# Four-layer graph network on one core: the third LSTM by seven products, an eigenvalue search from both ends, and a smaller arena placed by lifetimes

## The chip, the cores and the metric

The kernel runs on one core of a Trainium2 chip. The metric is device time in microseconds (us) of one execution; three executions of the kernel before took 2150.63, 2154.74 and 2155.52 us, so the median is 2154.74 us. The profile comes from one profiled execution. Engines are named as the profile names them: PE is the matmul engine (PEld its weight loads), DVE the vector engine, ACT the scalar engine, POOL GpSimd, SP the engine that issues most DMAs.

## What is computed

The input x is 128 graphs of 64 nodes with 256 features, and adj is one 64x64 matrix for all of them; everything is fp32. Four layers follow each other, each of the form x = x + layer(relu(layernorm(x))).

- **Layer 0** multiplies twice by adj and a 256x256 weight with a relu behind each, and then runs LSTMs with p = 0, 1, 2, 3 over windows of p + 1 nodes. The last hidden state of a window replaces the window's last node. Each step computes four gates:

```python
g = x_t @ Wih.T + h @ Whh.T + bias
i, f, gg, o = jnp.split(g, 4, axis=-1)
c = sigmoid(f) * c + sigmoid(i) * tanh(gg)
h = sigmoid(o) * tanh(c)
```

- **Layer 1** is graph attention with four heads and an MLP. Its first mix uses `2 * L / lam_max - I`, where lam_max is the largest eigenvalue of adj.
- **Layer 2** is one attention over the graph.
- **Layer 3** multiplies by the eigenvectors U of a 64x64 normalized Laplacian that is made from adj: U^T x, two small dense layers, U times the result.

The eigenvectors depend on adj alone. The kernel computes them itself, once, beside layer 0.

## The kernel before

**Tiling.** The 8192 rows (128 graphs of 64 nodes) are 64 tiles of 128 rows. Layer 0 takes them in NG = 8 groups of 8 tiles (`layer0`, line 1309), layers 1 to 3 in 16 groups of 4 tiles (`layer1` to `layer3`, lines 1523 to 1660). The result of layer 0 goes to DRAM (`put`) and is fetched back by the later groups.

**A planner sets the order.** No operation is issued as the Python text reaches it. `Plan.record` (line 114) notes each with its engine, its group and what it depends on; `Plan.schedule` (line 227) then goes through a simulated time with costs written out in `Plan.cost` (line 176) and, for each engine, picks an operation that can start earliest, with `Plan.rank` (line 328) to break ties; `Plan.issue` (line 338) emits all of them, in that fixed order. That one line, 344, is therefore the line of nearly all rows of the profile. Each engine works through its own list in order on the chip. `window` (line 968) lets at most two groups of layer 0 be in flight, then one group of the later layers beside the last group of layer 0, then eight. The groups have numbers: 0 to 7 are layer 0, then WEIGHTS, ATTN and REST to REST + 15 (layers 1 to 3).

**The eigenvalue work is a group apart.** It has the group number EIG and is named the plan's `aside` group. Its PE operations have rank -2, ahead of all others; its operations on DVE, ACT and POOL have rank 1000, so they fill what the groups leave. `eig_decomp` (line 347) brings the Laplacian to tridiagonal form in 62 steps, finds the eigenvalues by a search that counts sign changes of a Sturm sequence (line 634: NSWEEP = 9 sweeps, each with KS = 7 points for 3 levels, 21 numbers wide, over 64 partitions), and then makes the eigenvectors. In a sweep a loop over the 64 rows runs three DVE operations on 21 numbers each:

```python
for k in range(N):
    V.tensor_mul(PL[:, k + 1, :], DXf[:, k, :], PL[:, k, :])
    if k:
        b = W([N, 3, KS], 'b', 2)
        V.tensor_mul(b, PL[:, k - 1, :].rearrange('p (l s) -> p l s', l=3), E2[:, :, k - 1:k].to_broadcast([N, 3, KS]))
        V.tensor_sub(PL[:, k + 1, :], PL[:, k + 1, :], b.rearrange('p l s -> p (l s)'))
```

**LSTM steps.** `lstm_step` (line 1213) is the plain form: for each of 2 halves of the hidden features and 4 gates, two products with Wih and two with Whh into one PSUM bank (only Wih in a window's first step), then one ACT activation per gate and half. `lstm_fast` (line 1261) is Strassen's scheme in Winograd's form: each gate needs seven products with Wih and seven with Whh instead of eight and eight, each on half of the columns. `pieces` (line 1245) makes four extra right-hand sides, on POOL from the inputs and on DVE from the hidden state; four extra weight sums per matrix are made once by POOL at the start (line 1078) and stand in the tile `sums`. Between the products ACT copies banks out and DVE adds them. Before, p = 1 and p = 2 use `lstm_fast` in all steps but their first (line 1367). For p = 3 a group has 256 columns (2 halves of 8 tiles with 16 windows), and all four steps use `lstm_step`.

**Buffers.** There are 12 "big" buffers of 128x1024 fp32. Further ones come free later: 10 in `arena` when all EIG work is done (line 963), and 2, 7 and 5 in `Whh3`, `sums` and `mids` when layer 0 is done (lines 964 to 966), 36 in all. Before, `eig_decomp` lays its tiles side by side in the arena (10240 numbers per partition), with rings for some (`W`, line 372) and one region of 4080 that the stages share (`scope`, line 365).

**End of a group of layer 0.** Input x is fetched again for the residual sum (line 1374). `plan.behind` (line 1373) holds this fetch until the operation `last` has been issued; before, that is the last one ahead of p = 3. Sixteen PE transposes and four DVE adds of 128x512 end the group.

Of the kernel before, what the change touches and what calls it, by code (L numbers as in the profile page):

```python
# [8 lines left out]
ALU = mybir.AluOpType  # L9
AF = mybir.ActivationFunctionType  # L10
AX = mybir.AxisListType
# [4 lines left out]
KROW = 6  # L16
NEIG = 4080
EPS = 2.0 ** -24
# [50 lines left out]
class Plan:  # L69
# [258 lines left out]
    def rank(self, op):  # L328
        if op.group == self.aside:
            return (-2 if op.eng == "PE" else 1000, op.index)  # L330
        if op.eng == "SP":
            return (op.group, 0, op.index)
        g = min(max(op.group - op.lead, 0), self.ends)
        if op.group < REST:
            return (g, -op.lead, op.index)
        return (g, 6 * max(op.group - g, 0) - op.path, op.index)
# [10 lines left out]
def eig_decomp(plan, room, adj, adjT, ident, idf, ones):  # L347
# [14 lines left out]
    kept = {}  # L362
    inner = Carver(room.cut(NEIG))

    def scope():
        inner.reset([0])
        return inner

# [3 lines left out]
    def W(shape, name, bufs=None):  # L372

        if bufs is None:
            bufs = 2 if shape[-1] < N or name == "lab" else 1
        ring = kept.setdefault((name, tuple(shape)), [])
        if len(ring) < bufs:
            ring.append(room.tile(shape))
        else:
            ring.append(ring.pop(0))  # L380
        return ring[-1]

# [54 lines left out]
    V.memset(E[:, N - 1:N], 0.0)  # L437
    ph = scope()
    vb = [ph.tile([N, 2 * N]) for i in range(2)]
# [188 lines left out]
    C = 3 * KS  # L628
    ph = scope()
    PL = ph.tile([N, N + 1, C])  # L630
    V.memset(PL[:, 0, :], 1.0)
    DX = ph.tile([N, N, 3, KS])
    SG = ph.tile([N, N + 1, C])
    for s_ in range(NSWEEP):
        V.tensor_scalar(w, w, 1.0 / (KS + 1), None, op0=ALU.mult)
        x = W([N, 3, KS], 'x')
        V.tensor_scalar(x, c['ramp'], w, None, op0=ALU.mult)
        V.tensor_add(x, x, lo.unsqueeze(2).to_broadcast([N, 3, KS]))
        for l in range(3):
            V.tensor_mul(DX[:, :, l, :], BM[:, l, :].unsqueeze(2).to_broadcast([N, N, KS]), x[:, l, :].unsqueeze(1).to_broadcast([N, N, KS]))  # L640
            V.tensor_sub(DX[:, :, l, :], DM[:, l, :].unsqueeze(2).to_broadcast([N, N, KS]), DX[:, :, l, :])
        DXf = DX.rearrange('p k l s -> p k (l s)')
        for k in range(N):
            V.tensor_mul(PL[:, k + 1, :], DXf[:, k, :], PL[:, k, :])
            if k:
                b = W([N, 3, KS], 'b', 2)
                V.tensor_mul(b, PL[:, k - 1, :].rearrange('p (l s) -> p l s', l=3), E2[:, :, k - 1:k].to_broadcast([N, 3, KS]))
                V.tensor_sub(PL[:, k + 1, :], PL[:, k + 1, :], b.rearrange('p l s -> p (l s)'))
            if k % 8 == 7 and k < N - 1:
                mm = W([N, C], 'mm')  # L650
                V.tensor_reduce(mm, PL[:, k:k + 2, :].rearrange('p k c -> p c k'), op=ALU.max, axis=AX.X, apply_absolute_value=True)
                V.tensor_scalar(mm, mm, 1e-30, None, op0=ALU.max)
                V.reciprocal(mm, mm)
                V.tensor_mul(PL[:, k:k + 2, :], PL[:, k:k + 2, :], mm.unsqueeze(1).to_broadcast([N, 2, C]))
        V.tensor_scalar(SG, PL, 0.0, None, op0=ALU.is_lt)
        NE = DXf
        V.tensor_tensor(NE, SG[:, 1:, :], SG[:, :N, :], op=ALU.not_equal)
        ct = W([N, 3, KS], 'ct')
        V.tensor_reduce(ct.rearrange('p l s -> p (l s)'), NE.rearrange('p k c -> p c k'), op=ALU.add, axis=AX.X)
        V.tensor_tensor(ct, ct, li.unsqueeze(2).to_broadcast([N, 3, KS]), op=ALU.is_le)  # L660
        sm = W([N, 3], 'sm')
        V.reduce_sum(sm, ct, axis=AX.X)
        V.scalar_tensor_tensor(lo, sm, w, lo, op0=ALU.mult, op1=ALU.add)
# [6 lines left out]
    V.tensor_sub(dx, DM, dx)  # L670
    ph = scope()
    DQ = ph.tile([N, N, 2, 3])
# [202 lines left out]
    for _ in range(2):  # L875
# [8 lines left out]
        V.tensor_copy(Vc, pn[:N, N:2 * N])  # L884
    return AQf[:, N:], Vcf[:, :N], scope()

# [8 lines left out]
SETUP, WEIGHTS, ATTN, REST, EIG = -1, NG, NG + 1, NG + 2, 1000  # L895
NBIG, NMID, NSTAT, NATTN = 12, 10, 14, 4

# [32 lines left out]


@with_exitstack
def gnn_kernel(ctx: ExitStack, tc: tile.TileContext, a, out):
# [7 lines left out]

    arena = C([P, 10240], "arena")
    wih = [C([P, 2 * (3 if p == 0 else 4) * D], f"Wih{p}") for p in range(4)]
    whh = [None] + [C([P, 8 * D], f"Whh{p}") for p in range(1, 4)]
    sums = C([P, 2 * 7 * 4 * P], "sums")
    mids = C([P, NMID * 512], "mids")
# [130 lines left out]
    fastw = {}  # L1077
    for p in (1, 2):
        fastw[p] = []
# [24 lines left out]
    Ublk, UTblk = blockdiag(Ub), blockdiag(UTb)  # L1104
    room = Carver(arena)

    def colsum(col):

        pt = bank("colsum")
        PE.matmul(pt[:, :1], ones, col, start=True, stop=True)  # L1110
        r = room.tile([P, 1])
        V.tensor_copy(r, pt[:, :1])
        return r

    lam_j, lam_s = room.tile([N, N]), room.tile([P, 1])
    V.memset(lam_s, 0.0)

    def frob(m):
        V.scalar_tensor_tensor(lam_j, m, 1.0, m, op0=ALU.mult, op1=ALU.mult, accum_out=lam_s[:N])
        r = colsum(lam_s)  # L1120
        V.tensor_scalar(r, r, 1e-30, None, op0=ALU.max)
        G.tensor_tensor(r, r, mhalf[:, :1], op=ALU.pow)
        return r[:N]

    sym = room.tile([N, N])
    V.tensor_add(sym, adj2[:N], adjT2[:N])
    V.tensor_scalar(sym, sym, 0.5, None, op0=ALU.mult)
    Sf = room.tile([P, P])
    V.memset(Sf, 0.0)
    S = Sf[:N, :N]  # L1130
    V.scalar_tensor_tensor(S, sym, frob(sym), ident[:N, :N], op0=ALU.mult, op1=ALU.add)
    for i in range(21):
        pt = bank("lam_sq")
        PE.matmul(pt[:, :N], Sf, Sf[:, :N], start=True, stop=True)
        V.tensor_copy(S, pt[:N, :N])
        if i % 3 == 2:
            V.tensor_scalar(S, S, frob(S), None, op0=ALU.mult)
    V.scalar_tensor_tensor(lam_j, sym, 1.0, S, op0=ALU.mult, op1=ALU.mult, accum_out=lam_s[:N])
    lmax = colsum(lam_s)
    V.scalar_tensor_tensor(lam_j, S, 1.0, ident[:N, :N], op0=ALU.mult, op1=ALU.mult, accum_out=lam_s[:N])  # L1140
    den = colsum(lam_s)
    V.reciprocal(den, den)
    V.tensor_scalar(lmax, lmax, den, 1e-8, op0=ALU.mult, op1=ALU.add)
    V.reciprocal(lmax, lmax)
    V.tensor_scalar(lmax, lmax, 2.0, None, op0=ALU.mult)
    V.scalar_tensor_tensor(lapb, adjTb, lmax, ident, op0=ALU.mult, op1=ALU.subtract)


    QT, Vc, inner = eig_decomp(plan, room, adj2[:N], adjT2[:N], ident[:N, :N], ident, ones)
    for dst, lhs, rhs in ((Ublk, QT, Vc), (UTblk, Vc, QT)):  # L1150
        l2 = inner.tile([P, 2, N])
        V.tensor_copy(l2, lhs.unsqueeze(1).to_broadcast([P, 2, N]))
        pp = bank("U")
        PE.matmul(pp[:, :N], l2.rearrange("p r n -> p (r n)"), rhs, start=True, stop=True)
        V.tensor_copy(dst[0], pp[:N, :N])
        V.tensor_copy(dst[1], pp[N:, :N])

# [86 lines left out]

    def pieces(B, eng):

        n = B(0, 0).shape
        w = 1
        for k in n[1:]:
            w *= k  # L1250
        t = plan.value("big")[:, :4 * w].rearrange("p (i n) -> p i n", i=4)
        t = [t[:, i] for i in range(4)]
# [8 lines left out]
    def lstm_fast(p, xs, hs, cs, w, dsts):  # L1261


        R = [pieces(xs, G), pieces(hs, V)]
        sg = {}
# [43 lines left out]
    def layer0(fetched):  # L1309
# [47 lines left out]
        for p in range(1, 4):  # L1357
            k = p + 1
            nw = N // k
            if p == 3:  # L1360
                last = plan.ops[-1]
            for s in range(k):
                def win(c):
                    return hT[c].rearrange("p (b n t) -> p b n t", b=2, t=GT)[:, :, s:s + (nw - 1) * k + 1:k, :]
                ncol = 2 * GT * nw
                dst = win if s == p else lambda c: hs[:, c, :ncol]
                if s and p in (1, 2):
                    w = ncol // 2
                    lstm_fast(p, lambda c, n: win(c)[:, n], lambda c, n: hs[:, c, n * w:(n + 1) * w], cs, w, dst)
                else:  # L1370
                    lstm_step(p, s, win, hs, cs, ncol, dst)
# [55 lines left out]
    V.tensor_scalar(nb3a, nb3a, -1.0, None, op0=ALU.mult)  # L1427
    ursum = room.tile([P, 1])
    V.reduce_sum(ursum, Ub, axis=AX.X)
    V.tensor_scalar(b3b, b3b, ursum, None, op0=ALU.mult)  # L1430
    C3 = room.tile([P, P])
    pt = bank("ur")
# [279 lines left out]
```

## Time and profile before

| | us |
|---|---|
| median of three executions | 2154.74 |
| lowest, highest | 2150.63, 2155.52 |
| profiled execution: span from first to last instruction | 2149.3 |
| PE busy | 2102.0 (98%) |
| PE weight loads busy | 1665.0 (77%) |
| DVE busy | 1796.7 (84%) |
| ACT busy | 1124.1 (52%) |
| POOL busy | 708.4 (33%) |

For the profiled execution nothing but its span is given; the three timed executions lie 1.3 to 6.2 us above that span.

How to read it. The trace has two MATMUL records for one fp32 product and one for a transpose. [...] "Busy" is the time in which at least one record ran. A row of the table by form reads: line, engine, operation, output<-inputs, tile size, shapes, count, then busy us and mean ns of one, then the idle time of the engine ahead of these instructions and what ended it. A row of the table by stretches reads: from:to, its length, then PE, PEld, DVE, ACT and POOL with their busy us and counts, then the granted PE clock, the DMA share and GB/s. "big", "sums", "Wih" and other names are tiles; a later stage reuses such tiles under their old names, so `bank<-Whh,mids 128x128` is a product of layer 3.

### The profile page before, as it was taken

The numbers are of one execution on the slowest core, as the hardware profiler recorded it, in microseconds if no ns is written. First come the engines' busy times: TensorE is split into PE (matmuls) and PEld (weight loads), VectorE is DVE, ScalarE is ACT, GpSimd is POOL, SyncE is SP. The second block draws the span as 40 slices with busy tenths as digits, with TensorE's granted clock in tenths as the row PEclk, the third lists the DMA queues.
The fourth block names the chain that finished last, engine by engine and source line by source line (L and its number), as shares of the span: only waits on it lengthen the run. The fifth ranks groups of instructions, "written<-read, shape, count | busy, mean of one in ns | idle before, by whom it ended". The sixth has DMA issues, their size and how long they took to land.

```text
span 2149.3 us, 46200 instructions
## 1 busy us (share of the span) xinstructions
PE 2102.0 (98%) x16772; PEld 1665.0 (77%) x16772; DVE 1796.7 (84%) x7434; ACT 1124.1 (52%) x2465; POOL 708.4 (33%) x1040
## 2 busy tenths in 40 slices
PE   9999999999999999999999999999999999999998
PEld 6688688688778778778778788877777877887776
DVE  5788888888999999989989898767787789876787
ACT  3354354355345345345345444566667666665783
POOL 7211211310110110110110002696556657864353
PEclk9999999999999999999999999999999999999999
DMA  5000100100100100100000111200000100000001
GB/s 206 1 3 22 42 2 22 41 1 21 40 1 21 40 1 21 40 1 21 26 1 21 50 40 51 90 1 2 21 22 21 41 22 21 11 12 11 2 2 60
DMA packets 44868, 57.70 MB, mean 27 GB/s; under 512 B 8928, under 2 KB 38496, under 8 KB 44640
## 3 DMA queue, kind: packets, MB, share of 16 engines
q1 hardware_dynamic: 43536, 53.71, 7.6%
q8 instruction: 131, 2.15, 0.4%
q10 hardware_dynamic: 1104, 1.05, 0.2%
q14 instruction: 97, 0.79, 0.1%
HBM read 37.53 MB, written 16.78 MB: 25 GB/s over the span
## 4 chain that ended last, share of the span: by engine, by line
PE 79%; DVE 11%; POOL 3%; issue 3%; ACT 2%; DMA 2%; SPq 0%; DVEq 0%; ACTq 0%; POOLq 0%
PE bank L344 79%; DVE stat L344 3%; DVE arena L344 3%; DVE big L344 3%; POOL stat L344 2%; DVE mids L344 1%; DVE sums L344 1%; DMA big<-in_x_dram 1%; ACT big L344 1%; ACT mids L344 1%; POOL arena L344 0%; ACT arena L344 0%; POOL big L344 0%; DVE Whh L344 0%; SPq L344 0%
## 5 line engine op out<-in xcount | busy, mean ns | idle before, releaser
L344 PE MATMUL bank<-big,Wih 128*128 128x256 f32 (+3 forms) x2408 | 731.7, 426 | 14.7 <-DVE arena L344 6.9
L344 PEld LDWEIGHTS bank<-big,Wih 128*128 128x128 f32 x2408 | 440.3, 190 | 183.0 <-issue 100.2
L344 ACT ACTIVATE mids<-bank,bl 128x256 f32<-128x256 f32 (+3 forms) x528 | 274.8, 527 | 385.7 <-PE bank L344 383.3
L344 PE MATMUL bank<-big,Whh 128*128 128x256 f32 (+2 forms) x1692 | 448.0, 366 | 1.5 <-DVE big L344 1.4
L344 DVE TENSOR_TENSOR arena<-arena 64x21 f32<-64x21 f32 (+5 forms) x2253 | 372.3, 195 | 29.5 <-POOL arena L344 1.2
L344 PEld LDWEIGHTS bank<-big,Whh 128*128 128x128 f32 x1692 | 306.8, 190 | 40.6 <-issue 8.6
L344 PE MATMUL bank<-big,sums 128*128 128x168 f32 (+2 forms) x1472 | 263.8, 321 | 1.6 <-ACT big L344 1.5
L344 POOL TENSOR_SCALAR stat<-stat 128x4 f32<-128x4 f32 (+1 forms) x228 | 69.8, 307 | 514.0 <-DVE stat L344 499.2
L344 PEld LDWEIGHTS bank<-big,sums 128*128 128x128 f32 (+1 forms) x1472 | 220.5, 185 | 17.4 <-issue 3.4
L344 ACT COPY mids<-bank 128x168 f32<-128x168 f32 (+2 forms) x427 | 146.2, 364 | 151.9 <-PE bank L344 146.0
L344 DVE TENSOR_TENSOR big<-mids 128x512 f32<-128x512 f32 (+2 forms) x256 | 141.5, 562 | 33.9 <-ACT mids L344 30.7
L344 ACT ACTIVATE mids<-mids,bl 128x336 f32<-128x336 f32 (+3 forms) x192 | 102.1, 539 | 78.7 <-DVE mids L344 74.9
L344 DVE TENSOR_TENSOR mids<-bank,mids 128x168 f32<-128x168 f32 (+2 forms) x322 | 116.1, 368 | 25.1 <-PE bank L344 17.6
L344 DVE SCALAR_TENSOR_TENSOR arena<-arena 64x1 f32<-64x1 f32 (+15 forms) x565 | 124.3, 243 | 6.1 <-POOL arena L344 2.5
L344 POOL TENSOR_TENSOR stat<-stat,mhalf 128x4 f32<-128x4 f32 (+1 forms) x114 | 123.9, 1088 | 5.6
L344 ACT ACTIVATE mids<-big 128x256 f32<-128x256 f32 (+2 forms) x176 | 89.4, 510 | 62.7 <-DVE big L344 46.3
L344 POOL TENSOR_TENSOR big<-big 128x168 f32<-128x168 f32 (+1 forms) x30 | 21.4, 726 | 272.5 <-DVE arena L344 105.7
L344 DVE TENSOR_SCALAR arena<-arena 64x1 f32<-64x1 f32 (+8 forms) x533 | 102.4, 199 | 8.3 <-POOL arena L344 0.4
L344 DVE TENSOR_TENSOR big<-big,mids 128x256 f32<-128x256 f32 (+2 forms) x194 | 95.2, 492 | 9.7 <-ACT mids L344 8.5
L344 PE MATMUL bank<-Wih,big 128*128 128x256 f32 x384 | 94.1, 383 | 3.1 <-DVE big L344 0.9
L344 POOL TENSOR_TENSOR arena<-arena 64x1 f32<-64x1 f32 (+1 forms) x70 | 46.8, 669 | 145.9 <-ACT arena L344 105.8
L344 ACT ACT_TABLE_LOAD x55 | 70.6, 1283 | 35.9 <-PE bank L344 18.0
(371 smaller groups left out, 3747.9 us busy)
## 6 DMA issues: line engine op xcount, KB each, us to landing
big<-in_x_dram SPq DMA_DIRECT2D x30, 512.0 KB, 5.5
put<-big SPq DMA_DIRECT2D x16, 512.0 KB, 2.8
arena<-put SPq DMA_DIRECT2D x8, 512.0 KB, 6.6
out_dram<-arena SPq DMA_DIRECT2D x16, 256.0 KB, 2.3
Wih<-in_WihT_dram SPq DMA_DIRECT2D x3, 1024.0 KB, 11.9
Whh<-in_WhhT_dram SPq DMA_DIRECT2D x3, 1024.0 KB, 13.9
big<-put SPq DMA_DIRECT2D x5, 512.0 KB, 5.4
out_dram<-big SPq DMA_DIRECT2D x10, 256.0 KB, 2.2
```

The source lines that it names most:

```text
L344: getattr(self.engines[op.eng], name)(*map(real, args), **{k: real(a) for k, a in kw.items()})
```

## The change

1. **LSTM 3 by seven products.** Steps 1 to 3 of p = 3 use `lstm_fast`, as p = 1 and 2 do. Its products are 128 columns wide. The four weight sums of Wih3 and three of Whh3 (the fourth overwrites a block of Whh3) take another 7 x 512 numbers of `sums`, and POOL makes them at the start. The two sets of `pieces` of p = 3 share one big buffer.
2. **Sturm counts from both ends.** Each sweep runs 32 steps instead of 64. One step advances the sequence from the top and the one from the bottom together, 42 numbers wide; after the last step the two halves are joined by a few operations. The tensors BM2, DM2 and EE hold the matrix folded in that way, and the six operations that fill DX become two of 64x1344.
3. **Eigenvalue tiles by lifetimes.** The eigenvalue work is now the function `spectrum`, called twice: first with `Lives`, which only notes when each tile is first and last used, then with the plan and with `Homes`, which gives each tile a place for its lifetime. The rings and the shared region are gone; the arena has 4992 numbers per partition and so gives 4 big buffers later.
4. **Buffers.** There are 14 big buffers from the start. `sums` gives 10 later instead of 7; in all there are 35.
5. **Order.** POOL operations of EIG get rank -2, as those of PE have. The fetch for the residual sum may go once the last step of p = 3 begins, where it could go before p = 3. The column sum of U and the tile C3 (for layer 3) belong to EIG, not WEIGHTS. `window` and `reserve` are as before.

The core of the diff:

```diff
     def rank(self, op):
         if op.group == self.aside:
-            return (-2 if op.eng == "PE" else 1000, op.index)
+            return (-2 if op.eng in ("PE", "G") else 1000, op.index)
...
-    PL = ph.tile([N, N + 1, C])
-    DX = ph.tile([N, N, 3, KS])
-    SG = ph.tile([N, N + 1, C])
+    PL = ph.tile([N, Hf + 1, 2 * C])
+    DX = ph.tile([N, Hf, 2 * C])
+    BM2, DM2, EE = both(), both(), both()
...
-        for l in range(3):
-            V.tensor_mul(DX[:, :, l, :], BM[:, l, :].unsqueeze(2).to_broadcast([N, N, KS]), x[:, l, :].unsqueeze(1).to_broadcast([N, N, KS]))
-            V.tensor_sub(DX[:, :, l, :], DM[:, l, :].unsqueeze(2).to_broadcast([N, N, KS]), DX[:, :, l, :])
-        for k in range(N):
-            V.tensor_mul(PL[:, k + 1, :], DXf[:, k, :], PL[:, k, :])
+        V.tensor_mul(DX4, wide(BM2), x.unsqueeze(1).to_broadcast([N, N, 3, KS]))
+        V.tensor_sub(DX4, wide(DM2), DX4)
+        for j in range(Hf):
+            V.tensor_mul(PL[:, j + 1, :], DX[:, j, :], PL[:, j, :])
+            if j:
+                b = W([N, 6, KS], 'b', 2)
+                V.tensor_mul(b, PL[:, j - 1, :].rearrange('p (l s) -> p l s', l=6), EE[:, 6 * j:6 * j + 6].unsqueeze(2).to_broadcast([N, 6, KS]))
+                V.tensor_sub(PL[:, j + 1, :], PL[:, j + 1, :], b.rearrange('p l s -> p (l s)'))
...
+        ends = W([N, 2, C], 'ends')
+        V.tensor_mul(ends, PL[:, Hf - 1:, :C], PL[:, Hf - 1:, C:])
+        V.tensor_mul(e0, e0, mid3)
+        V.tensor_tensor(ends[:, 0, :], ends[:, 1, :], ends[:, 0, :], op=ALU.is_lt)
...
-NBIG, NMID, NSTAT, NATTN = 12, 10, 14, 4
+NBIG, NMID, NSTAT, NATTN = 14, 10, 14, 4
...
+class Homes:
+    def __init__(self, arena, spans):
...
+        for i in sorted(range(len(spans)), key=lambda i: (-max(spans[i][2], 256), spans[i][0])):
+            a, b, n = spans[i]
+            busy = sorted((p, p + m) for d, p, m, c in placed if c < b and a < d)
...
-    arena = C([P, 10240], "arena")
+    arena = C([P, 4992], "arena")
-    sums = C([P, 2 * 7 * 4 * P], "sums")
+    sums = C([P, 3 * 7 * 4 * P], "sums")
...
-    for p in (1, 2):
+    for p in (1, 2, 3):
         fastw[p] = []
...
+    lives = Lives(arena)
+    spectrum(lives, lives)
+    homes = Homes(arena, lives.spans)
+    spectrum(plan, homes)
...
-        R = [pieces(xs, G), pieces(hs, V)]
+        both = plan.value("big") if 8 * w <= HT * D else None
+        R = [pieces(xs, G, both), pieces(hs, V, both and both[:, 4 * w:])]
...
-            if p == 3:
-                last = plan.ops[-1]
             for s in range(k):
+                if p == 3 and s == k - 1:
+                    last = plan.ops[-1]
...
-                if s and p in (1, 2):
+                if s:
                     w = ncol // 2
                     lstm_fast(p, lambda c, n: win(c)[:, n], lambda c, n: hs[:, c, n * w:(n + 1) * w], cs, w, dst)
...
-    ursum = room.tile([P, 1])
+    ursum, C3 = room.tile([P, 1]), room.tile([P, P])
+    plan.group = EIG
     V.reduce_sum(ursum, Ub, axis=AX.X)
```

## The prediction

> **What bounds the kernel now.** I read the busy times first, then the table by stretches, then the timeline of PE. The first says which engine is full, the second whether it is full in every stage, the third what one of its instructions costs.
>
> ```profile
> PE 2102.0 (98%) x16772; PEld 1665.0 (77%) x16772; DVE 1796.7 (84%) x7434; ACT 1124.1 (52%) x2465; POOL 708.4 (33%) x1040
> ```
> ```profile
> 34.00:1350.00 1316.00, 1299.17 (x7721) 1028.00 (x7722) 1152.81 (x5556) 597.11 (x1485) 198.70 (x347) 1.00 0.07 22
> 1350.00:2149.00 799.00, 773.76 (x8715) 615.85 (x8713) 624.04 (x1782) 519.23 (x963) 485.51 (x648) 1.00 0.07 23
> ```
> ```profile
> 556.00:720.00 164.00, 162.79 (x977) 128.33 (x976) 150.64 (x708) 72.88 (x165) 15.98 (x24) 1.00 0.06 20
> ```
>
> The kernel is bound by PE: 2102.0 of 2149.3 us, at the full granted clock. Layer 0 (34 to 1350 us) leaves PE idle for 16.8 us; one group of it takes some 162 us (third line) and leaves 1.2 idle. DVE is at 92% there, and the eigenvalue work fills it up: the instructions on arena tiles take 98.4 of its 150.64 us. So a product that is removed is worth its pace, if DVE and ACT keep up, and work taken from DVE is worth nothing by itself.
>
> Pace is read from start to start:
>
> ```profile
> 689.51 1.03 PE L344 MATMUL bank<-big,Wih 128*128 128x256 f32 x4
> 690.37 1.03 PE L344 MATMUL bank<-big,Whh 128*128 128x256 f32 x4
> ```
> ```profile
> 1518.47 1.95 PE L344 MATMUL bank<-Whh,mids 128*128 128x128 f32 x16
> 1520.25 0.60 PE L344 MATMUL bank<-Wih,arena 128*128 128x256 f32 x2
> ```
>
> The first pair is LSTM 3 itself: four records, that is two products of 256 columns, in 0.863 us (689.51 to 691.23 is two such steps), 0.432 us each. The second pair is layer 3, the only fp32 stage with 128 columns, and each product there has new weights, as the seven products have: eight in 1.78 us, 0.2225 each.
>
> **The change part by part.**
>
> *PE.* A plain step of p = 3 is 2 halves x 4 gates x 4 products = 32 of 256 columns; a fast one is 4 gates x 14 = 56 of 128. With 3 steps in 8 groups, 768 products of 256 go and 1344 of 128 come; the counts of the two instruction lists say the same, and no other PE form changes its count. Removed: 768 x 0.432 = 331.8 us. Added: 1344 x 0.2225 = 299.0 us. A line through the paces at 168 columns (0.286) and 256 gives 0.2196 at 128, 295.1 us. So PE loses 32.8 to 36.7 us; I take 34, near the measured row, as these products stand in long runs as the 168-column ones do.
>
> [...] The records of 128 columns follow each other at 0.111 us, those of 256 at 0.216, although each weight load is recorded with 190 ns: the loads overlap. [...]
>
> *The wait between steps.* This is what can eat the gain. A plain step starts with 16 products of Wih (6.9 us) that don't need the hidden state, so its wait is hidden. In a fast step every bank mixes Wih and Whh from its first burst on, so the step waits for ACT, two DVE multiplications and four `pieces`. The trace has this wait at the two fast steps of p = 2:
>
> ```profile
> 653.43 0.45 PE L344 MATMUL bank<-big,Whh 128*128 128x168 f32 x2
> 653.72 3.02 PE L344 MATMUL bank<-big,Wih 128*128 128x512 f32 x8
> 653.92 0.40 ACT L344 ACTIVATE mids<-bank,bl 128x168 f32<-128x168 f32 x1 [0.24 <-PE bank L344]
> ...
> 655.97 0.33 DVE L344 TENSOR_TENSOR big<-big,big 128x168 f32<-128x168 f32 x1
> 656.21 0.68 DVE L344 TENSOR_TENSOR big<-mids 128x512 f32<-128x512 f32 x1
> ...
> 656.58 0.45 PE L344 MATMUL bank<-big,Whh 128*128 128x168 f32 x2
> ```
>
> From the last product (653.72) to the first of the next step (656.58) are 2.86 us, and PE fills them with 512-column products of the next group. p = 3 gets three such places per group, 24 in all: 24 x 2.86 = 69 us if nothing covered them. The instruction list of the changed kernel shows the cover: in groups 0 to 6 three to six products of 512 columns (0.86 us each, so 2.6 us and more) stand around each of the 21 places, most of them split over its last products, and where those run out, products of p = 1 of the next group follow. A group has 36 of them (24 of p = 0, 12 of p = 1's first step), which is enough. In group 7 no such group follows: one place has only five transposes (0.6 us) and two have some 3 us of layer 1. I charge 2.3 us for the first and 0.1 us for each of the others: 4.6 us. Bounds: 0 and 69.
>
> *ACT and DVE in a fast step.* Four gates x 14 x 0.221 = 12.4 us of PE. ACT, from its rows at 168 and 256 columns carried on to 128: 12 copies of 0.26, 8 sigmoids or tanh of 0.36, 4 of 0.506 and 2 tanh of 0.41 make 8.9 us. DVE paces 168 columns at 0.24 (650.90 to 651.14 above the lines shown) and 256 at 0.34, so 128 at 0.20: 16 more operations are 3.2 us per step, 77 us over 24 steps, and the step has 5.9 us with its old ones. Both lie below 12.4. POOL gets 96 pieces at about 0.5 us (168 columns: 0.588), 48 us on an engine at 33%. All this lies beside PE.
>
> *Sturm sweeps.* DVE only.
>
> ```profile
> L344 DVE TENSOR_TENSOR arena<-arena 64x21 f32<-64x21 f32 x1728 | 242.2, 178 | 17.0
> ...
> L344 DVE TENSOR_TENSOR arena<-arena 64x42 f32<-64x42 f32 x63 | 13.1, 208 | 1.6
> ```
>
> 1728 operations at a pace of 0.13 to 0.15 us become 864, each longer by 0 to 0.03 us (the difference of 178 and 208 ns): 224 to 259 us become 112 to 156, some 100 saved; 27 renormalizations of about 1 us fall away, less what the other 36 grow: 20. With the added 77, DVE does about 45 us less. On the path that is worth nothing: PE was not waiting for it. What it buys is that DVE isn't overfull: without it layer 0 would need 1153 + 77 = 1230 us of DVE in some 1280. With it, the last eigenvalue operation on DVE stands at the start of p = 2 of group 7, some 80 us of PE work (p = 2 and 3) before that group ends, where before it stood in its last step.
>
> *Setup.* POOL makes seven more sums and one in place, 8 x 1.27 = 10.2 us (the 128x512 `sums<-Wih` row), first needed at LSTM 3 of group 0, some 130 us in. Hidden; if POOL's statistics of group 1 queue behind them, up to 3 us.
>
> *Buffers and order.* 35 instead of 36 buffers; 10 arena buffers freed at 1347 us become 4, freed earlier. The late residual fetch still has the last step (12.4 us and its cover) for a transfer of 5.5 us. POOL's rank for EIG shortens a chain that nothing waits for, and a wait for a reused place in the arena would fall on that same chain (POOL already waits 270.4 us for DVE and 105.8 for ACT there, off the path). The PE lists of the last 330 rows are the same in form and order. Nearest rows: PE waits 25 us in 1350 to 2149; I let this move by 5 us either way, and take 0. In the passage from layer 0 to the rest (1200 to 1400 us) PE lost some 14 us, 2 to 4 of them on eigenvalue results; these go: -3.
>
> *Sum.* 2149.3 - 34 + 4.6 - 3 = 2117 us of span. The median of the runs shown lies 5.4 us above the span; I keep that: 2122 us.
>
> **The rivals.**
>
> *The step wait shows (slower).* The list's cover is planned, not measured. If each of the 24 places cost its 2.86 us, the span would be 2149.3 - 34 + 69 = 2184, the median 2189. It decides at 34 / 24 = 1.4 us per place: above that the change loses. For it: fast steps of p = 3 are shorter than those of p = 2, with the same chain. Against: at p = 2 the same cover leaves nothing idle, and there is 1.2 us of idle in a whole group.
>
> *DVE or ACT runs late (part of the gain is lost).* DVE stays some 90% full in layer 0, and now twelve of its operations per fast step release PSUM banks that PE waits for; a 64x1344 reduction takes 3.08 us. One lost stall of 0.5 to 1.2 us per fast step costs 12 to 29 us: 2134 to 2151, say 2142.
>
> *Idle falls too (better).* With eigenvalues done one stage sooner, layer 1 can start earlier beside group 7: of the 11 us left at the passage and 8 x 1.2 us in the groups, half to three quarters could go, 10 to 15 us: 2107 to 2112, say 2109.
>
> *It doesn't do what it says* (128 columns paced by the 190 ns loads): +179 us. The rows at 0.111 us exclude it.
>
> **How the numbers follow.** Forecast, 2112 to 2132: 0.66. Idle falls too, 2100 to 2112: 0.10. DVE or ACT late, 2132 to 2150: 0.16. Step wait, 2150 to 2189: 0.08. 0.2% (4.3 us, about what a measurement of this kernel can tell from no change) around 2154.74 is 2150.4 to 2159.1: of the last case 0.03 falls within, 0.05 above. Faster 0.92, same 0.03, slower 0.05. The range 2104 to 2143 leaves out the whole last case, 0.06 of the third and 0.04 of the second: 0.18.
>
> **What would show it.** Products of 128 columns in runs at 0.219 to 0.223 us; PE busy near 2068; PE idle between 40 and 55 us. Between the fast steps of p = 3, 512-column products and then no wait above 0.3 us for DVE or ACT. The 64x42 operations at a pace below 0.18. The last eigenvalue copy (UTb) before 1250 us. Wrong would be: PE waiting for `mids` or `big` of DVE in each p = 3 step, or a 128-column pace above 0.23.

## The result, and the profile after

| | before | changed |
|---|---|---|
| median, us (4 executions each) | 2154.22 | 2167.95 |
| lowest, highest | 2150.63, 2155.52 | 2166.83, 2169.99 |
| profiled execution: span | 2149.3 | 2168.2 |

The ratio of the times is 1.0067, with a 95% interval of 1.0055 to 1.0080: 0.7% slower, where 1.5% faster had been forecast, and 25 us above the end of the range.

The busy times of the changed kernel, and its table by the stretches that were shown of before (from:to, length, busy us and counts of PE, PEld, DVE, ACT and POOL, then the granted clock):

```profile
PE 2092.7 (97%) x17924; PEld 1684.8 (78%) x17924; DVE 1794.0 (83%) x6861; ACT 1196.0 (55%) x2835; POOL 766.2 (35%) x1144
```
```profile
34.00:1350.00 1316.00, 1286.14 (x8838) 1043.33 (x8837) 1150.25 (x4959) 680.28 (x1856) 271.73 (x458) 0.99 0.07 22
1350.00:2168.00 818.00, 777.75 (x8740) 619.42 (x8738) 619.48 (x1792) 507.22 (x960) 473.05 (x642) 0.98 0.07 22
556.00:720.00 164.00, 159.87 (x1101) 127.27 (x1100) 154.43 (x624) 82.96 (x208) 28.07 (x38) 1.00 0.05 17
```

PE idles 29.9 us in the first stretch (16.8 before), 40.3 in the second and 4.1 in the one group (1.2 before). The clock column is new: 0.99 and 0.98, where it was 1.00. The waits of PE (us in total, times, longest):

```profile
PE bank L343 <- DVE big L343: 15.7, 17, 2.6
PE bank L343 <- DVE mids L343: 10.4, 9, 4.4
PE bank L343 <- POOL big L343: 9.1, 2, 8.8
PE bank L343 <- ACT mids L343: 8.9, 6, 4.6
```

Single waits of 4.4, 8.8 and 4.6 us stand there. In before no wait was longer than 2.7:

```profile
PE bank L344 <- ACT mids L344: 7.1, 7, 2.7
```

**A measure of loss.** Busy time doesn't tell a slow product from a fast one: from 742.90 to 746.30 us PE is busy for all of the 3.40 us, with 11 records at a granted clock of 0.51. So I took, for every matmul record, the time to the start of the next one less the pace that its shape has when nothing disturbs it (0.110 us for 128 columns, 0.216 for 256, 0.429 for 512), and added these up. Work and loss together make the span, to some 6 us. "Start" is the first 60 us of PE work, "layer 0" goes on to the last 168-column product (p = 2 of group 7), "passage" is the next 110 us of work, "later" the rest.

| us | work | start | layer 0 | passage | later |
|---|---|---|---|---|---|
| before | 2054.4 | 14.9 | 29.7 | 8.3 | 36.5 |
| changed | 2016.9 | 24.7 | 51.0 | 18.7 | 51.1 |
| difference | -37.5 | +9.8 | +21.3 | +10.4 | +14.6 |

The differences add up to +18.6; the spans differ by 18.9. (The medians differ by 13.7, so some 5 us of this table belong to the two executions that were profiled.) What the products gained was lost one and a half times over.

The 0.110 us of this measure is a little too small for the new products. They take 0.223 us each, that is 0.1115 for each of their two records, as the next rows show. So 1344 of them take 299.7 us, for 331.8 us removed, and the work fell by 32 us rather than by 37.5. The other 5 us stand in the table as loss, in every kernel with fast steps of p = 3, and nearly all of them in layer 0, where 21 of the 24 fast steps run.

**The products and the step wait were as forecast.** PE at the end of a step of p = 3 in group 2:

```profile
549.08 0.39 PE L343 MATMUL bank<-big,Whh 128*128 128x128 f32 x2
549.30 2.10 PE L343 MATMUL bank<-big,Wih 128*128 128x512 f32 x6
551.25 0.39 PE L343 MATMUL bank<-big,Whh 128*128 128x128 f32 x2
551.47 1.02 PE L343 MATMUL bank<-big,Wih 128*128 128x512 f32 x2
```

Products of 128 columns start 0.223 us apart (5th to 95th percentile: 0.223 to 0.224), and 512-column products of the next group fill the wait: no row has an idle time in brackets behind it.

**Where it was not.** The start. All engines but PEld, from 51 us on:

```profile
51.18 1.26 POOL L343 TENSOR_TENSOR Whh<-Whh 128x512 f32<-128x512 f32 x1
...
52.10 6.46 DVE L343 SCALAR_TENSOR_TENSOR arena<-arena 64x1 f32<-64x1 f32 x1
52.40 1.26 POOL L343 TENSOR_TENSOR sums<-Whh,sums 128x512 f32<-128x512 f32 x1
...
57.29 1.25 POOL L343 TENSOR_TENSOR sums<-Whh 128x512 f32<-128x512 f32 x1
58.48 0.67 DVE L343 TENSOR_TENSOR mids<-bank,nB 128x512 f32<-128x512 f32 x1
...
59.21 1.56 PE L343 MATMUL bank<-adjTb,mids 64*64 64x64 f32 x48 [4.42 <-DVE mids L343]
```

A DVE instruction on one number per partition, 0.20 us elsewhere, lasts 6.46: it ends when POOL's run of sums, one behind the other without a gap, ends at 58.54. Behind it stands the evacuation (58.48) that PE waits for. Another such instruction took 3.01 us from 21.26. Over the first 100 us DVE instructions last some 15 us longer in all than the medians of their forms; in before it is some 5.

The passages. PE at the start of group 6, and at the passage to layer 1:

```profile
898.96 3.60 PE L343 MATMUL bank<-big,Wih 128*128 128x512 f32 x8
907.18 2.82 PE L343 MATMUL bank<-adjTb,mids 64*64 64x64 f32 x64 [4.63 <-ACT mids L343]
```
```profile
1362.17 0.59 PE L343 MATMUL bank<-Wih,big 128*128 128x256 f32 x2
1362.60 0.39 PE L343 MATMUL bank<-big,sums 128*128 128x128 f32 x2
...
1367.50 1.16 PE L343 MATMUL bank<-arena,big 64*64 64x64 f32 x64
1377.45 1.12 PE L343 MATMUL bank<-ident,big 128*128 128x128 f32 x4 [8.79 <-POOL big L343]
```

The first mix of group 6 waits for layernorm statistics, with no product left to run beside it. At 1362 products of layer 1 (`bank<-Wih,big`) stand between the 128-column ones of the last fast step; at 1368 none is left, and PE waits for a softmax of REST 0.

The clock. Three of the nine stretches at half clock, each in or just behind a wait of PE, and the wait ahead of the first of the three:

```profile
742.90:746.30 3.40, 3.40 (x11) 2.77 (x10) 3.40 (x7) 0.37 (x1) 0.00 (x0) 0.51 0.21 86
906.70:916.90 10.20, 8.70 (x78) 6.79 (x79) 7.18 (x17) 5.81 (x13) 3.03 (x4) 0.50 0.01 2
1370.90:1381.10 10.20, 3.65 (x71) 3.21 (x72) 10.20 (x42) 4.48 (x8) 6.36 (x9) 0.50 0.97 353
```
```profile
741.53 1.76 PE L343 MATMUL bank<-ident,big 128*128 128x128 f32 x12 [1.98 <-DVE big L343]
```

From 34 us to the last products the granted clock is half for 3.41 us or a multiple of it each time, 51 us in all; in before it was 3.41 us. A 256-column record took 0.427 us at 743 in place of 0.216.

### The profile page after: what moved, and what is told of

It reads as the page before. It is cut to its first block, busy times and chain, and to the rows that moved or that the text cites. A ratio compares the mean times of both kernels' runs of the same rounds, so it can differ in the third digit from the quotient of the medians.

```text
span 2168.2 us, 48732 instructions
## 1 busy us (share of the span) xinstructions
PE 2092.7 (97%) x17924; PEld 1684.8 (78%) x17924; DVE 1794.0 (83%) x6861; ACT 1196.0 (55%) x2835; POOL 766.2 (35%) x1144
## 5 line engine op out<-in xcount | busy, mean ns | idle before, releaser
L343 PE MATMUL bank<-big,Wih 128*128 128x256 f32 (+4 forms) x2184 | 633.3, 403 | 4.7 <-DVE mids L343 4.3
L343 PE MATMUL bank<-big,sums 128*128 128x128 f32 (+3 forms) x2944 | 456.0, 296 | 0.6 <-ACT mids L343 0.6
L343 PEld LDWEIGHTS bank<-big,sums 128*128 128x128 f32 (+1 forms) x2944 | 391.8, 186 | 26.9 <-issue 12.0
L343 PE MATMUL bank<-big,Whh 128*128 128x128 f32 (+4 forms) x1804 | 398.7, 316 | 7.5 <-DVE big L343 7.2
L343 ACT COPY mids<-bank 128x128 f32<-128x128 f32 (+3 forms) x719 | 220.3, 321 | 244.4 <-PE bank L343 233.6
L343 ACT ACTIVATE mids<-bank,bl 128x512 f32<-128x512 f32 (+4 forms) x432 | 217.6, 514 | 202.4 <-PE bank L343 197.8
L343 PEld LDWEIGHTS bank<-big,Whh 128*128 128x128 f32 (+1 forms) x1804 | 278.5, 190 | 31.9 <-issue 10.8
L343 DVE TENSOR_TENSOR arena<-arena 64x42 f32<-64x42 f32 (+6 forms) x1359 | 276.0, 230 | 16.1
L343 ACT ACTIVATE mids<-mids,bl 128x256 f32<-128x256 f32 (+4 forms) x384 | 187.2, 496 | 135.5 <-DVE mids L343 131.2
L343 DVE TENSOR_TENSOR mids<-bank,mids 128x128 f32<-128x128 f32 (+2 forms) x609 | 194.3, 325 | 67.3 <-PE bank L343 47.2
## 6 DMA issues: line engine op xcount, KB each, us to landing
Whh<-in_WhhT_dram SPq DMA_DIRECT2D x3, 1024.0 KB, 13.7
```

The source lines that it names most:

```text
L343: getattr(self.engines[op.eng], name)(*map(real, args), **{k: real(a) for k, a in kw.items()})
```

## The experiments

My first theory, T: the seven products are worth their 36 us, but the step waits of p = 3 use up the 512-column products that used to cover the passages, and the bare waits halve the clock. Rival R1: the rest of the change (buffers, places, POOL's rank) costs the time. One part of R1, POOL's rank, came out as the largest single effect, so T alone is not the cause.

All times and losses are in one table. Times are medians of 4 to 10 executions. Ratios are to executions of before that were made beside them, with medians of 2152.53 to 2154.05, so a difference between two kernels carries up to 1.5 us of that. The losses are those of one profiled execution of each.

| kernel | us | ratio, 95% interval | start | layer 0 | passage | later |
|---|---|---|---|---|---|---|
| no_lstm3 | 2184.1 | 1.0144 [1.0127, 1.0161] | 20.5 | 27.6 | 7.8 | 65.5 |
| no_rank | 2141.5 | 0.9948 [0.9933, 0.9963] | 13.3 | 45.0 | 20.6 | 37.6 |
| win3 | 2142.0 | 0.9948 [0.9933, 0.9963] | 19.4 | 21.0 | 26.6 | 52.9 |
| keep | 2160.2 | 1.0031 [1.0018, 1.0044] | 18.2 | 34.2 | 7.9 | 38.5 |
| nl_norank | 2183.4 | 1.0145 [1.0130, 1.0160] | 15.4 | 33.6 | 7.8 | 66.9 |
| rank_late | 2141.5 | 0.9948 [0.9933, 0.9963] | 13.0 | 43.7 | 23.9 | 35.5 |
| before_rank | 2168.1 | 1.0074 [1.0058, 1.0091] | 24.0 | 35.7 | 8.5 | 36.2 |
| win3_norank | 2125.4 | 0.9872 [0.9857, 0.9886] | 13.5 | 20.7 | 22.8 | 45.8 |
| nl_oldpools | 2150.0 | 0.9982 [0.9973, 0.9992] | 15.3 | 25.9 | 7.8 | 39.3 |
| no_sums | 2157.5 | 1.0022 [1.0013, 1.0032] | 14.9 | 48.9 | 25.6 | 42.5 |
| no_sums_nr | 2144.0 | 0.9955 [0.9939, 0.9972] | 15.3 | 32.7 | 26.7 | 45.6 |
| before_win3 | 2148.8 | 0.9982 [0.9973, 0.9992] | 14.1 | 14.9 | 13.7 | 44.0 |
| nl_16big | 2162.7 | 1.0037 [1.0022, 1.0052] | 15.3 | 41.3 | 7.8 | 37.8 |
| nl_15big | 2188.4 | 1.0163 [1.0148, 1.0179] | 15.3 | 36.7 | 7.8 | 66.7 |
| win3_nl_norank | 2168.1 | 1.0070 [1.0053, 1.0087] | 14.4 | 16.5 | 7.5 | 68.0 |

**POOL's rank.**

```diff
no_rank (from the changed kernel; before_rank is the reverse edit, made to before):
-            return (-2 if op.eng in ("PE", "G") else 1000, op.index)
+            return (-2 if op.eng == "PE" else 1000, op.index)
rank_late:
+            return (-2 if op.eng == "PE" or op.eng == "G" and (op.index > 274 or 134 < op.index < 195) else 1000, op.index)
no_sums (leaves the 24 sums out, plain quadrants stand in for them; no_sums_nr: with no_rank's line as well):
-            G.tensor_tensor(s1, a21, a22, op=ALU.add)
...
-            fastw[p].append({1: a11, 2: a12, 3: s4, 4: a22, 5: s1, 6: s2, 7: s3})
+            fastw[p].append({1: a11, 2: a12, 3: a12, 4: a22, 5: a21, 6: a11, 7: a21})
```

> Undoes one part: eigenvalue work on POOL ranks last again, all else as changed. Theory T: the rank moves only a chain off the path, 2163 to 2173. Rival R1 with POOL's order as its mechanism (eigenvalue instructions now go ahead of the statistics that the mix of the next group and REST wait for): the stalls of 4.6, 4.8 and 9.0 us at 54, 902 and 1368 us shrink and the half clock behind them goes, 2140 to 2155.

> As changed, but the eigenvalue instructions on POOL that the plan put in the first 50 us (15 of 149) rank last again; all later ones stay first. Theory P (the rank's price is paid at the start: the early eigenvalue chain brings DVE instructions with two SBUF inputs beside POOL's run of sums, and they stand until the run ends: one 64x1 instruction that takes 0.20 us elsewhere took 6.46 us from 52.10, another 3.01 us from 21.26, and PE's mix of group 1 waits 4.6 us behind them): the start gets back its 12 to 14 us, so 2142 to 2156, and DVE's excess in the first 100 us falls from 14.8 to some 4 us. Rival Q (the rank hurts all along, by POOL serving eigenvalues ahead of the statistics in each group and by another order in the later layers): 2162 to 2170.

> The kernel before with one edit, the rank of eigenvalue work on POOL. Theory A/P (separate price, at the start): 2153 + 8 to 15 = 2161 to 2168, DVE instructions held beside POOL's sums in the first 60 us. Theory B (only with LSTM 3's added sums): 2150 to 2156. If it is above 2170, the rank costs in the later layers too.

> As changed, rank and all, but the 24 sums of weight quadrants that POOL makes at the start are left out (the fast steps take plain quadrants in their place, the same number and shape of products). Theory P (the rank's price at the start is DVE standing beside POOL's back-to-back sums): no DVE instruction held for over 1.5 us in the first 100 us, PE's loss in its first 60 us of work falls from 24.7 to 13 to 16 us, and the time is 2140 to 2152, within 6 us of the same kernel without the rank. Rival O (bringing the eigenvalue chain forward costs by its order on PE and DVE alone): the loss stays above 20 us and the time at 2160 to 2170.

> The same without the sums, and with the eigenvalue work on POOL last again: the control for the run above. Both theories: within 5 us of 2141.5, as the sums lie beside other work there.

no_rank gives 26.4 us back: the rank alone is more than the whole loss of 13.7. T, which said 2163 to 2173, is wrong here. rank_late gives back all of it by 15 of 149 instructions, those of the first 50 us. no_sums, at 2157.5, missed P's range. The stretch from 18 to 80 us, in the changed kernel, no_rank and no_sums, one line each:

```profile
18.00:80.00 62.00, 54.01 (x542) 34.16 (x542) 45.11 (x131) 15.47 (x37) 45.02 (x48) 0.94 0.28 104
```
```profile
18.00:80.00 62.00, 61.17 (x558) 35.84 (x557) 36.99 (x130) 20.39 (x44) 46.22 (x49) 1.00 0.28 103
```
```profile
18.00:80.00 62.00, 61.26 (x591) 39.27 (x590) 47.67 (x233) 20.24 (x53) 19.39 (x33) 1.00 0.27 100
```

With rank and sums PE idles 8 us there; with either away, 0.8. At the start the rank costs something only where POOL makes sums: 11.4 and 5.9 us of loss with 24 sums (changed against no_rank, win3 against win3_norank), 9.1 and 5.1 with 16 (before_rank against before, no_lstm3 against nl_norank), -0.4 with none, where no DVE instruction of the first 100 us lasts longer than 1.1. That is theory P, for the start, though the size does not follow the number of sums. In the changed kernel eight DVE instructions of the first 100 us last over 0.5 us longer than the median of their form, and all eight read two tiles in SBUF. The one of 6.46 us lasted through six POOL instructions. Why an instruction stands like that wasn't shown.

But the start is not all. In the four pairs with sums, in the order above, the rank costs 26.4, 16.6, 15.6 and 0.7 us of time; it moves layer 0 by 6.0, 0.3, 6.0 and -6.0 us of loss, and the later layers by 13.5, 7.1, -0.3 and -1.4. Without sums it still costs 13.5 us, 16 of loss in layer 0. So it is neither a price by itself, which before_rank alone would suggest, nor one that needs LSTM 3's sums, which nl_norank alone would suggest. I read the rest as a new order: the eigenvalue chain runs earlier, DVE's long instructions meet other passages, and the planner's list comes out another way. That is argued; what is shown is that the rest, too, hangs on the 15 early instructions, as rank_late gives all of it back. I can show what costs the start its time; why the rest fell as it did stays open.

**The cover.**

```diff
win3 (win3_norank: with no_rank's line; before_win3: on before; win3_nl_norank: with no_lstm3's lines as well):
-        return max(oldest, 0) + 2 - oldest if oldest < NG - 1 else REST + 1 - oldest if oldest < REST else 8
+        return max(oldest, 0) + 3 - oldest if oldest < NG - 1 else REST + 1 - oldest if oldest < REST else 8
no_lstm3 (nl_norank: with no_rank's line):
-    for p in (1, 2, 3):
+    for p in (1, 2):
...
-                if s:
+                if s and p in (1, 2):
```

> Undoes one part: LSTM 3 runs with plain steps again (768 products of 256 columns in place of 1344 of 128); the new sweep, the places by lifetimes, the buffers and POOL's rank stay as changed. Theory T (the fast steps of LSTM 3 use up the 512-column products that used to cover the passages between groups and from layer 0 to layer 1; bare stalls of some 2 us and more then halve the granted clock): PE gets 36 us of work back, loses about 30 us of stalls and 22 us of half clock, 2168 + 36 - 52 = 2152, range 2146 to 2162, with next to no half clock between 60 and 2100 us. Rival R1 (buffers, places and POOL's order cost it, whatever LSTM 3 does): the stalls and the half clock stay and the work comes back, 2168 + 36 = 2204, range 2190 to 2210. In between, the two share it: each us below 2204 is LSTM 3's.

> One number changed: three groups of layer 0 in flight instead of two (window oldest + 3), all else as changed. Theory T: the 512-column products of the group after next cover the passages again; the planner's own list of PE gaps shrinks from 113 to 85 us, and the half clock of layer 0 (24 us of it at half, 12 lost) goes: 2168 - 28 - 8 = 2132, range 2120 to 2145. Rival R1 (the loss sits in REST, for want of buffers): only the passages of layer 0 gain, and three groups hold more buffers: 2155 to 2175.

> Undoes two parts: LSTM 3 plain and eigenvalue work on POOL last again; new sweep, places and buffers stay. So the four kernels (as changed 2168, without LSTM 3's products 2184, without the rank 2141.5, without both) tell how the two add up. Theory A (they are separate prices): 2184 - 26.5 = 2158, and the products are worth 16 us either way, not 36. Theory B (the rank hurts by the sums that LSTM 3 adds to POOL at the start, so only together): 2178 to 2184, and the products are worth 36 to 42 us without the rank.

> As changed, with three groups of layer 0 in flight and the eigenvalue work on POOL last again. If the cover that LSTM 3 eats and the rank are two separate prices: 2168 - 26 - 26.5 = 2115.5, range 2108 to 2122, faster than both kernels. If the third group in flight had bought back the rank's price (the same stalls): 2132 to 2142.

> The kernel before with one number changed, three groups of layer 0 in flight. If the third group only repairs the cover that LSTM 3's fast steps use up, before has little to gain: layer 0 loses 20 us of PE there against 14 in the changed kernel with three groups, so 2145 to 2152. If it is worth 16 to 26 us by itself: 2127 to 2137, and LSTM 3's products would be worth nothing on top of it.

> Three groups in flight, rank undone, LSTM 3 plain. With the cover there, the seven products should be worth their pace: layer 0 (up to the last step of LSTM 3 in group 7) 30 to 36 us longer than in win3_norank. Of the total I expect more, 2125 + 33 + up to 25 for the later layers with 35 buffers: 2158 to 2184. If the products' gain were the accident of a better list in the later layers, layer 0 would differ by less than 15 us.

One stretch of layer 0 in the changed kernel, in no_rank and in win3_norank, one line each:

```profile
560.00:820.00 260.00, 253.84 (x1788) 200.88 (x1787) 242.01 (x929) 128.00 (x318) 40.38 (x56) 0.99 0.07 21
```
```profile
560.00:820.00 260.00, 256.41 (x1822) 206.15 (x1821) 241.78 (x945) 129.06 (x323) 40.43 (x57) 1.00 0.07 21
```
```profile
560.00:820.00 260.00, 259.99 (x1853) 211.32 (x1852) 237.61 (x971) 135.41 (x340) 37.10 (x63) 1.00 0.07 21
```

With a third group in flight PE does not idle in this stretch, and layer 0's loss falls from 45.0 to 20.7 us (51.0 to 21.0 with the rank). These 24 us are not all LSTM 3's doing: the same edit takes 14.8 us off layer 0 in before (29.7 to 14.9 in before_win3), so cover was missing there already. Four kernels without the rank price what the fast steps add. (Their total times don't: with plain steps and 35 buffers the later layers lose some 28 us more, as the next part shows. no_lstm3 fell between both theories.) The last 168-column product of group 7 stands behind 21 of the 24 fast steps of p = 3; it starts at 1295.9 us in win3_nl_norank and at 1264.5 in win3_norank. That is 31.4 us, 1.50 per step; the forecast was 34 / 24 = 1.42, and the paces give 32.1 / 24 = 1.34. With two groups in flight it is 1314.0 against 1291.0, so 23: 8 us, a quarter of the gain, go to bare waits of layer 0. That is T's part. The fast step of p = 3 also costs 13 to 15 us in the passage (7.8 to 20.6, and 7.5 to 22.8 with three groups): group 7 fills its step waits with products of REST 0, and then REST 0's softmax stands bare, for 8.8 us in the changed kernel and 10.0 in no_rank.

before gains 4.4 us by the third group: most of its 15 us in layer 0 are lost again later. win3_norank missed its 2115.5 (rank and window share some of their 26 us each), but at 2125.4 us it is the fastest of all: 1.3% faster than before (0.9872 [0.9857, 0.9886]), and 42.5 us below the changed kernel.

**The buffers.** nl_norank was the surprise: without the fast steps of p = 3 and without the rank it should have been near before, and it is 31 us slower.

```diff
nl_oldpools (from nl_norank; 36 buffers in all):
-NBIG, NMID, NSTAT, NATTN = 14, 10, 14, 4
+NBIG, NMID, NSTAT, NATTN = 12, 10, 14, 4
-    arena = C([P, 4992], "arena")
+    arena = C([P, 10240], "arena")
-    sums = C([P, 3 * 7 * 4 * P], "sums")
+    sums = C([P, 2 * 7 * 4 * P], "sums")
nl_16big (the same, but; 36 in all. nl_15big: with 15, so 35):
+NBIG, NMID, NSTAT, NATTN = 16, 10, 14, 4
+    arena = C([P, 6144], "arena")
```

> Without LSTM 3's products and without the rank (2183.4 us), and with the buffers of before (arena 10240, sums for two LSTMs, 12 big): what is left of the change is the new sweep and the places by lifetimes. Theory B (the 31 us between 2152.5 and 2183.4 are the price of fewer spare buffers in the later layers, where PE lost 28 us in before and 59 here): 2150 to 2160. Rival (they come from the sweep and the places, which give DVE's eigenvalue work another order): 2175 to 2186.

> Without LSTM 3's products and without the rank, with 16 large buffers of their own, 6 from the arena and 7 from the sums: 36 in all as in before, but of other kinds and with an arena little larger than the changed kernel's. If the number decides: 2146 to 2156, as with the buffers of before (2150). If the arena's ten buffers and the time they come free decide: 2172 to 2184, as with the changed kernel's (2183).

> The same with 15 large buffers of their own in place of 16, 35 in all as in the changed kernel. If the number decides: 2172 to 2184, that is 25 us and more for one buffer, and PE's loss in the later layers rises from about 30 to 55 us or more. If not: within 5 us of nl_16big.

So the sweep, the places by lifetimes and the later fetch are worth 3 us together, beside plain steps of p = 3 (nl_oldpools against before, 0.9982 [0.9973, 0.9992]); the later fetch wasn't tried alone. One buffer is worth 25.6 (nl_15big against nl_16big), all of it in the later layers, where the four kernels with 35 buffers and plain LSTM 3 lose 65.5 to 68.0 us and the five with 36 lose 36.2 to 44.0. The number is not all: nl_16big fell between its two forecasts, some 12 us above nl_oldpools with the same 36, and loses 41.3 us in layer 0 for 25.9. The later layers of nl_16big, then of nl_15big, seen from 1400 to 2100 us, PE idle 12.2 and 26.4:

```profile
1400.00:2100.00 700.00, 687.84 (x7468) 541.95 (x7472) 550.00 (x1549) 468.91 (x864) 434.05 (x573) 1.00 0.05 14
```
```profile
1400.00:2100.00 700.00, 673.62 (x7111) 529.52 (x7112) 531.56 (x1474) 436.63 (x819) 419.28 (x555) 0.99 0.05 14
```

With LSTM 3's products in, 35 buffers lose only 35.5 to 52.9 there: the later layers then start in another state. That this state is the reason isn't shown, nor why one buffer helps so much; the products with 36 buffers were not run.

**The clock.**

```diff
keep: in issue(), ahead of 17 waiting operations
+    for i in range(n):
+        self.engines["PE"].matmul(self.pools["bank"][v.buf][:, :128], self.ones, self.ones, start=True, stop=True)
```

> As changed, but PE is given 168 more products of ones (128 columns, 0.2225 us each, some 37 us in all) just ahead of the 17 longest stalls, into a bank that the waiting instruction overwrites, each time some 0.2 to 0.5 us less than the stall lasted. Theory of the clock (behind a stall of about 2 us and more the granted clock halves for 3.4 to 10.2 us, and that is 21 to 25 us of the time): the stretches at half clock fall from 51 us to under 15, mean clock above 0.995, 2168 - 20 = 2148, range 2143 to 2156. Rival: the clock falls for another reason, or is no loss because PE waits there anyhow: 2165 to 2180.

The clock is back at 0.998 and the time falls by 7.8 us, outside the range of both sides. Record by record against the changed kernel, keep is ahead by 1.9 us behind the first half-clock stretch (6.83 us long), and gains 0.7, 1.7 and 3.3 more at those of 251, 743 and 907 us (3.41, 3.41, 10.24), nothing in between; in the later layers it gains 2.4 in all. So half clock costs 8 to 10 us (the medians differ by 7.8, the profiled executions by 9.9) of the 20.9 that PE loses in the nine stretches. The rest didn't come back; that PE would have waited elsewhere is the likely reason, but isn't shown.

## Why the prediction was wrong

- *PE, -34.* Right: the products go at 0.223 us each, 299.7 us for the 1344, which makes -32.1, and where the cover is there they bring 1.50 us per step for 1.42.
- *The wait between steps, +4.6.* The 21 places themselves are covered, as the text said, with few exceptions (a wait of 1.84 us before 696.0). The step that failed is "which is enough": a group's 36 wide products were counted against the step waits of p = 3 alone. They had been covering other waits of layer 0. There no_rank, which has no rank in it, lost 15.3 us more than before; some 5 of these are the pace of the measure, and some 10 are bare waits, in place of 4.6. With three groups in flight fast steps cost layer 0 nothing beyond that pace (20.7 in win3_norank for 16.5 in win3_nl_norank).
- *Passage, -3.* With plain LSTM 3 the passage loses 7.8 in place of 8.3, so little of the 3 us was to be had. But the list showed that two places of group 7 are filled with layer 1's products, and I did not ask what those products had been covering: +12.3 (no_rank).
- *POOL's rank, 0.* "Shortens a chain that nothing waits for" is the largest failure: 26.4 us. The chain's end is waited for by nothing, but its instructions stand in DVE's queue, and moved to the first 50 us they stand beside POOL's sums and ahead of layer 0's evacuations. That shows for the 11.4 us of the start; how the others come about is open.
- *Setup, 0 to 3.* The eight sums cost nothing that shows: the start loses 13.3 in no_rank for 14.9 in before, and with the rank 24.7 for 24.0 in before_rank, which has sixteen sums.
- *Buffers and order, 0 ± 5.* For the changed kernel without the rank it held (later 37.6 for 36.5), but by luck: the same buffers cost about 28 us with plain LSTM 3, and the rank moved this stretch by 13.5. The bound of 5 us had no row behind it.
- *Half clock.* Not in the sum at all: 8 to 10 us, part of the losses named above.
- *DVE.* 64x42 operations go at a median of some 0.12 us (forecast below 0.18), but DVE's busy time fell by 2.7 and not by 45 us, in no_rank by 21. The last copy to UTb stands at 1265 us, not before 1250.
- *The rivals.* The slower side was given 0.08, for bare step waits at p = 3. The cover did run out, at another place than it named; and nothing in the cases had the rank.

Without the rank the sum missed by 22 us (a span of 2139.0 in no_rank, 2117 in the forecast): some 15 in the passage, some 6 in layer 0, 2 in the products. So 2141.5 us would have been just inside the range, 19.5 above the forecast, with two of its terms wrong.

## What to carry to other kernels

Cover is a stock: before new waits are filled with an engine's spare products, ask which other waits these products were covering, and try more work in flight if there are any. A priority given to a chain off the path is not free: it moves the chain's instructions in every queue that they share, and should be tried by itself. Where a greedy list sets the order, small edits move distant stages: here one buffer moved the later layers by 29 us of loss and one rank by 13. So each edit of a bundle is measured alone, and in more than one surrounding: the same rank cost 26.4 us in one kernel and 0.7 in another.

## What the runs showed of the hardware

- A DVE instruction on SBUF tiles that starts while POOL runs can stand until POOL's whole run of back-to-back instructions ends: 6.46 us for one of 0.20 (changed kernel, from 52.10), 3.01 for one of 0.27 (from 21.26). It isn't always so: in no_rank one of 64x64 at 53.60 got in and was done after 0.80 us, beside sums that follow each other as closely.
- The granted clock halved behind waits of PE shorter than the stretch it then lasted: in the changed kernel 1.98 us before 741.5 brought 3.41 us of half clock, 4.63 before 907.2 brought 10.24. It isn't certain: 1.84 us before 696.0 brought none, nor did 2.19 (before 232.1) and 2.69 us (before 894.6) in the kernel before.
